# Attention sums of a graph layer on halves and quarters of TensorE's columns

## The chip, the cores and the metric

The kernel runs on one core of one Trainium2 chip. A core has a matrix engine (TensorE, PE in the profile; PEld are its weight loads), a vector engine (DVE), a scalar engine (ACT), GpSimd (POOL) and SyncE (SP), and DMA queues that SP, ACT and POOL issue to. The metric is the device time in microseconds of the core. Before the change the median of three runs is 1650.38 us (1650.38 to 1653.8).

## The reference, cut to what matters

The layer is a graph attention block followed by a mixture of eight expert networks, of which each token uses two. Everything is float32. The change concerns the attention:

```python
h = jnp.einsum('nd,hdk->hnk', x, W)                 # 4096 nodes, 4 heads, 64 columns each
s_col = jnp.einsum('hnk,hk->hn', h, a1)
s_row = jnp.einsum('hnk,hk->hn', h, a2)
e = jax.nn.leaky_relu(s_row[:, :, None] + s_col[:, None, :], negative_slope=0.2)
e = jnp.where(adj[None, :, :] > 0, e, NEG_INF)
att = jax.nn.softmax(e, axis=-1)
h_prime = jnp.einsum('hij,hjk->hik', att, h)
out = jnp.transpose(h_prime, (1, 0, 2)).reshape(N, OUT_DIM)
y = jax.nn.elu(out) + residual                      # then a layer norm
...
# experts: gate, top 2 of 8, gelu(xf @ W1[e] + b1[e]) @ W2[e] + b2[e], weighted sum
```

For each head and each node i the kernel needs two sums over the neighbours j: the sum of weight times row of h (64 numbers), and the sum of the weights (one number), by which the first is divided.

## The kernel before, in words

The 4,096 nodes i are cut into 8 blocks of 512 (B), and the neighbours j into 32 tiles of 128 (P). Block by block, `load_mask` brings a piece of the transposed adjacency matrix and turns it into a mask of zeros and ones on ACT (L778, L779). For each tile j, `weigh` makes four tiles w of 128 x 512 on DVE, one per head, with one instruction each (L786): the larger of a row term `er` and a column term `eb`, times the mask. These w rotate through ten buffers. `attend` then runs one matmul per head (L507): the stationary operand is `ha[:, j, h, :]`, 128 x 65, which holds the 64 columns of h scaled by a factor `ed` and, as column 65 (K1 = 65), the factor itself; the moving operand is w[h]; the result accumulates over the 32 tiles j in `acc[h]`, 65 partitions x 512 in one bank of PSUM per head. Row 65 of the result is the sum of weights. Each float32 matmul is carried out as two passes, each with its own weight load, so that the profile counts 2,048 where the program has 8 x 32 x 4 = 1,024.

In block 0 the norm of x (`norm_block`, transposes at L402) and the projections (`project_block`, L422 and L446, which also writes `ha`) are done tile by tile beside the attention. At the end of a block, `finish_block` copies the four accumulators from PSUM to `u` (two on ACT at L643, two on DVE at L645), transposes them in pieces of 65 x 128 back to nodes on partitions (L651, sixteen per block), copies each group of four to `raw` on ACT (L654), divides by the sum of weights (L659 to L667), and goes on with elu, residual, layer norm and routing (`route_block`). `finish_block` is a generator: its pieces are issued between tiles j of the next block, and those of the last block between pieces of the experts' work. The experts' stage (`up`, L889, and `down`, L902) reuses the PSUM banks acc0 to acc2 by turns for `up` and acc3 and ph for `down`.

There are two branches for the attention. The one under `general > 0` serves large scores; with these inputs the other one runs, and all lines of the profile are from it. Inside a branch a scheduler decides the order of the instructions on each engine from the program text, so that pieces of other work stand between the matmuls of L507. Each engine then works through its own list strictly as listed, and semaphores hold an instruction until what it reads is there or what it overwrites has been read.

The steps of the prediction touch `attend` (L505 to L509), `project_block` (L437), `finish_block` (L641 to L667), `up` (L886) and `down` (L900).

Of the kernel before, what the change touches and what calls it, by code (L numbers as in the profile page):

```python
# [9 lines left out]
F32 = mybir.dt.float32  # L10
# [3 lines left out]
OP = mybir.AluOpType  # L14
# [3 lines left out]
P = 128  # L18
# [9 lines left out]
TT = CH * NCH  # L28
# [9 lines left out]
def gat_then_moe(  # L38
# [19 lines left out]
    nc = tc.nc  # L58
    N, D = x.shape
    H, _, K = W.shape  # L60
    E, _, F = W1.shape
    NT = N // P
    DC = D // P
    FC = F // P
    B = 512
# [8 lines left out]

    W_1, W_2, ID, FIRST, RW = D, D + 1, D + 2, D + 3, D + 4
    TB = B // P
    K1 = K + 1
    HK = H * K

    const = ctx.enter_context(tc.tile_pool(name="const", bufs=1))  # L80
    small = ctx.enter_context(tc.tile_pool(name="small", bufs=3))
# [250 lines left out]
    with ExitStack() as layer:  # L332
# [46 lines left out]
        nc.vector.tensor_scalar(flag, wide, 0.5 * SPREAD, None, op0=OP.is_gt)  # L379


        ha = gat.tile([P, NT, H, K1], F32)
        sums = gat.tile([P, DC, NB], F32)
        eb = gat.tile([P, NT, H], F32)
        acc = [ps.tile([K1, B], F32, tag=f"acc{h}", name=f"acc{h}") for h in range(H)]

        turned = {}

# [21 lines left out]
        def project_block(b, apart):  # L410

            xT = turned[b]
            sc = small.tile([P, TB, 2 * H], F32, tag="sc", name="sc")
            rb = front.tile([P, TB, D], F32, tag="rb", name="rb", bufs=1)
            here = slice(b * TB, (b + 1) * TB)
            cols, rows = sc[:, :, :H], sc[:, :, H:]
            if not apart:
                nc.vector.memset(ha[:, here, :, K : K + 1], 1.0)
            for t in range(TB):
                ph = ps.tile([P, HK + 2 * H], F32, tag="ph", name="ph")  # L420
                for c in range(DC):
                    nc.tensor.matmul(  # L422
                        ph, xT[:, c, ts(t, P)], wall[:, c, :],
                        start=(c == 0), stop=(c == DC - 1),
                    )
                mine = ha[:, b * TB + t, :, :K]
                h4 = ph[:, :HK].rearrange("p (h k) -> p h k", h=H)
                if apart:
                    nc.vector.tensor_tensor(
                        sc[:, t, :H], ph[:, HK : HK + H], limit, OP.subtract  # L430
                    )
                    nc.vector.tensor_tensor(
                        sc[:, t, H:], ph[:, HK + H :], limit, OP.add
                    )
                    ed = ha[:, b * TB + t, :, K]
                    nc.scalar.activation(ed, sc[:, t, :H], AF.Exp, scale=SLOPE)
                    nc.vector.tensor_tensor(  # L437
                        mine, h4, ed.unsqueeze(2).to_broadcast([P, H, K]), OP.mult
                    )
                else:  # L440
                    nc.vector.tensor_copy(sc[:, t, :], ph[:, HK:])
                    nc.scalar.copy(mine, h4)
                if t % 2 == 0:
                    pr = ps.tile([P, 2, D], F32, tag="pr", name="pr")
                for c in range(DC):
                    nc.tensor.matmul(  # L446
                        pr[:, t % 2, :], xT[:, c, ts(t, P)], wr[:, c, :],
                        start=(c == 0), stop=(c == DC - 1),
                    )
                if t % 2:  # L450
                    nc.vector.tensor_tensor(
                        rb[:, t - 1 : t + 1, :], pr,
                        brm.unsqueeze(1).to_broadcast([P, 2, D]), OP.add,
                    )
            nc.gpsimd.dma_start(rows_of(residual, b), rb)

            part = small.tile([P, H, TB], F32, tag="part", name="part")
            turn = part.rearrange("p h t -> p t h")
            if apart:
                nc.scalar.activation(eb[:, here, :], cols, AF.Exp, scale=1.0 - SLOPE)  # L460
                nc.vector.tensor_scalar(turn, rows, 0.0, None, op0=OP.max)
                nc.scalar.activation(part, part, AF.Exp, scale=SLOPE - 1.0)
            else:
                nc.vector.tensor_copy(eb[:, here, :], cols)
                nc.vector.tensor_copy(turn, rows)
            pp = ps.tile([H * TB, P], F32, tag="ph", name="pp")
            nc.tensor.transpose(pp, part.rearrange("p h t -> p (h t)"), ident)
            sp = small.tile([H * TB, P], F32, tag="sp", name="sp")
            nc.scalar.copy(sp, pp)
            nc.gpsimd.dma_start(  # L470
                parts[:, ts(b, B)].rearrange("h (t p) -> h t p", p=P),
                sp,
            )
# [29 lines left out]
            return at  # L503

        def attend(w, j):  # L505
            for h in range(H):
                nc.tensor.matmul(  # L507
                    acc[h], ha[:, j, h, :], w[h], start=(j == 0), stop=(j == NT - 1)
                )  # L509

        def route_block(b, y):

# [118 lines left out]
        def finish_block(b):  # L631

            xb = fin.tile([P, TB, D], F32, tag="xf", name="xf", bufs=1)
            nc.sync.dma_start(xb, rows_of(x, b))
            nc.gpsimd.tensor_tensor(
                xb, xb, bet.unsqueeze(1).to_broadcast([P, TB, D]), OP.add
            )
            rb = fin.tile([P, TB, D], F32, tag="rb", name="rb", bufs=1)
            nc.sync.dma_start(rb, rows_of(residual, b))
            u = fin.tile([K1, H, B], F32, tag="u", name="u", bufs=1)  # L640
            for h in range(H):  # L641
                if h % 2 == 0:
                    nc.scalar.copy(u[:, h, :], acc[h])  # L643
                else:
                    nc.vector.tensor_copy(u[:, h, :], acc[h])  # L645
            yield
            raw = fin.tile([P, TB, H, K1], F32, tag="raw", name="raw", bufs=1)
            for t in range(TB):
                pt = ps.tile([P, H, K1], F32, tag="ptr", name="ptr", bufs=2)
                for h in range(H):  # L650
                    nc.tensor.transpose(  # L651
                        pt[:, h, :], u[:, h, ts(t, P)], ident[:K1, :K1]
                    )
                nc.scalar.copy(raw[:, t], pt)  # L654
                if t % 2:
                    yield
            shape = [P, TB, H, K]
            none = small.tile([P, TB, H], F32, tag="none", name="none")
            nc.vector.tensor_scalar(none, raw[:, :, :, K], 0.0, None, op0=OP.is_equal)  # L659
            z = small.tile([P, TB, H], F32, tag="z", name="z")  # L660
            nc.vector.tensor_tensor(z, raw[:, :, :, K], none, OP.add)
            nc.vector.reciprocal(z, z)
            y = fin.tile([P, TB, D], F32, tag="y", name="y", bufs=1)
            y4 = y.rearrange("p t (h k) -> p t h k", h=H)
            m = fin.tile([P, TB, D], F32, tag="m", name="m", bufs=1)
            m4 = m.rearrange("p t (h k) -> p t h k", h=H)
            nc.vector.tensor_tensor(  # L667
                y4, raw[:, :, :, :K], z.unsqueeze(3).to_broadcast(shape), OP.mult
            )
            nc.gpsimd.tensor_tensor(  # L670
                m4,
                hbar.unsqueeze(1).to_broadcast(shape),
                none.unsqueeze(3).to_broadcast(shape),
                OP.mult,
            )
            nc.gpsimd.tensor_tensor(y, y, m, OP.add)
            nc.vector.tensor_scalar(m, y, 0.0, None, op0=OP.min)
            nc.scalar.activation(m, m, AF.Exp)
            nc.vector.scalar_tensor_tensor(y, y, 0.0, m, op0=OP.max, op1=OP.add)
            yield  # L680
            nc.vector.tensor_tensor(y, y, rb, OP.add)
            yield
            mv, r = mean_rstd(y)
            for t in range(TB):
                nc.vector.scalar_tensor_tensor(  # L685
                    y[:, t, :], y[:, t, :], mv[:, t, 0:1], gam,
                    op0=OP.subtract, op1=OP.mult,
                )
            for t in range(TB):
                nc.vector.scalar_tensor_tensor(  # L690
                    y[:, t, :], y[:, t, :], r[:, t : t + 1], xb[:, t, :],
                    op0=OP.mult, op1=OP.add,
                )
            nc.gpsimd.dma_start(rows_of(out, b), y)
            yield
            yield from route_block(b, y)
# [185 lines left out]
    def up(job, xT):  # L882

        hT = work.tile([P, FC, TT], F32, tag="hT", name="hT")
        for f in range(FC):
            ph = ps.tile([P, TT], F32, tag=f"acc{turns[0] % 3}", name="ph")  # L886
            turns[0] += 1
            for c in range(DC):
                nc.tensor.matmul(  # L889
# [6 lines left out]
    def down(job, hT):  # L896

        yT = work.tile([P, DC, TT], F32, tag="yT", name="yT")
        for c in range(DC):
            py = ps.tile([P, TT], F32, tag=("acc3", "ph")[c % 2], name="py")  # L900
            for f in range(FC):
                nc.tensor.matmul(  # L902
                    py, job[2][:, f, ts(c, P)], hT[:, f, :],
# [101 lines left out]
```

## Time and profile before

| what | value |
|---|---|
| median of three runs | 1650.38 us |
| the profiled execution's own time, and its span | 1650.22 us, 1648.6 us |
| mean granted clock of TensorE | 0.981 |
| busy: PE, PE weight loads, DVE, ACT, POOL | 1541.9, 742.1, 1076.4, 485.5, 290.8 us |
| first and last start of the matmuls of L507 | 62.1 and 1049.3 us |
| busy in 60 to 1050 us: PE, DVE, ACT | 966.43, 917.00, 317.36 us |
| DMA over the span | 113 GB/s |

The span falls into two parts. From about 60 to 1050 us the attention runs; each block after the first takes about 119 us. From 1050 us on the experts run, with PE busy and DVE mostly idle. A group's row in the profile gives its line, engine, operation, tiles and shapes, then the busy time in us, the mean duration of one in ns, and the idle time of the engine just before it with what ended it. A matmul's duration includes the time until its result is out, which overlaps the next matmul: the busy time of the group is therefore less than count times mean.

### The profile page before, as it was taken

To read this page: it belongs to the slowest core of one execution; us is meant where nothing else is said; L and a number is where in the kernel's file an instruction comes from. 1 tells how busy PE (TensorE), PEld (TensorE's weight loads), DVE (VectorE), ACT (ScalarE), POOL (GpSimd) and SP (SyncE) were. 2 spreads that over 40 slices of the span, in tenths; PEclk is the share of its full clock that TensorE was granted. 3 is DMA by queue.
4 is the path that set the end of the run, shared out by engine and by line. 5 is a ranking of instruction groups with operands and counts; after the bars stand their busy time and mean duration, and the time that the engine had idled before them with its cause. 6 is when DMAs were issued, how large, how long until landed. Compare 5 with 4: busy or idle time off the path is not lost.

```text
span 1648.6 us, 14261 instructions
## 1 busy us (share of the span) xinstructions
PE 1541.9 (94%) x4886; PEld 742.1 (45%) x4886; DVE 1076.4 (65%) x2334; ACT 485.5 (29%) x611; POOL 290.8 (18%) x223
## 2 busy tenths in 40 slices
PE   4799999999999999999999999999499999999994
PEld 2354533333333333333333333467366666666662
DVE  4698789999999999899899899444111121221211
ACT  3343233332333223333323323343032222222220
POOL 1100010210210210211211111213412222222222
PEclk9899999999999999999999999999799999999997
DMA  5532223232332333423332311544565555566541
GB/s 171 142 118 89 77 77 115 93 111 90 105 112 91 112 92 102 126 68 105 126 102 94 96 64 42 188 140 111 139 184 136 135 138 136 141 155 153 154 109 20
DMA packets 120643, 187.93 MB, mean 114 GB/s; under 512 B 11525, under 2 KB 71877, under 8 KB 120557
## 3 DMA queue, kind: packets, MB, share of 16 engines
q1 hardware_dynamic: 92748, 148.03, 28.8%
q0 software_dynamic: 21120, 29.27, 8.2%
q10 hardware_dynamic: 6688, 9.58, 2.5%
q8 instruction: 42, 0.69, 0.2%
q14 instruction: 45, 0.36, 0.1%
HBM read 157.64 MB, written 29.18 MB: 113 GB/s over the span
## 4 chain that ended last, share of the span: by engine, by line
PE 77%; DVE 15%; DMA 4%; issue 1%; ACT 0%; POOLq 0%; POOL 0%; ACTq 0%; SPq 0%; DVEq 0%
PE acc L507 40%; PE ph L889 15%; PE py L902 15%; DVE w L786 9%; PE ph L422 2%; DMA out<-o,ids 1%; PE pr L446 1%; PE po L917 1%; DVE st L145 1%; DMA xb<-in_x 1%; PE pt L871 1%; PE pg L531 1%; DMA out<-y 1%; DVE y L690 1%; DVE y L685 1%
## 5 line engine op out<-in xcount | busy, mean ns | idle before, releaser
L507 PE MATMUL acc<-w,ha 128*65 128x512 f32 x2048 | 896.0, 594 | 21.9 <-DVE w L786 21.9
L786 DVE SCALAR_TENSOR_TENSOR w<-er,eb,am 128x512 f32<-128x512 f32 x1024 | 773.6, 776 | 48.7 <-PE acc L507 9.6
L507 PEld LDWEIGHTS acc<-w,ha 128*65 128x65 f32 x2048 | 277.5, 138 | 594.0 <-issue 360.1
L889 PE MATMUL ph<-xT,w 128*128 128x330 f32 x896 | 267.8, 447 | 5.5 <-DMA w<-in_L_ffn_W 3.4
L902 PE MATMUL py<-hT,w 128*128 128x330 f32 x896 | 255.8, 440 | 0.0
L778 ACT ACTIVATE am<-adj 128x2048 bf16<-128x2048 int32 x64 | 122.3, 1910 | 350.6 <-DVE w L786 348.1
L921 POOL DMA_INDIRECT out<-o,ids x84 | 133.3, 1586 | 406.5 <-DMA out<-o,ids 257.9
L902 PEld LDWEIGHTS py<-hT,w 128*128 128x128 f32 x896 | 168.6, 189 | 77.3
L889 PEld LDWEIGHTS ph<-xT,w 128*128 128x128 f32 x896 | 164.9, 191 | 76.5 <-issue 5.6
L906 DVE TENSOR_SCALAR yT<-py,bias 128x330 f32<-128x330 f32 x56 | 31.4, 561 | 246.7 <-PE py L902 246.7
L893 ACT ACTIVATE hT<-ph,bias 128x330 f32<-128x330 f32 x224 | 119.4, 536 | 166.2 <-PE ph L889 166.0
L626 POOL DMA_INDIRECT lists<-xe,at x64 | 73.8, 1152 | 341.1 <-DVE at L595 139.8
L779 ACT ACTIVATE am<-am 128x2048 bf16<-128x2048 bf16 x64 | 122.1, 1908 | 1.7
L875 ACT COPY xT<-pt 128x330 f32<-128x330 f32 x28 | 12.2, 434 | 238.7 <-PE pt L871 238.0
L918 DVE TENSOR_SCALAR o<-po,share 110x256 f32<-110x256 f32 x84 | 40.4, 481 | 39.1 <-PE po L917 39.0
L422 PE MATMUL ph<-wall,xT 128*128 128x264 f32 x128 | 36.9, 414 | 15.8 <-DVE ha L437 10.0
L670 POOL TENSOR_TENSOR m<-hbar,none 128x1024 f32<-128x1024 f32 x8 | 15.2, 1895 | 201.6 <-DVE none L659 201.6
L852 DVE TENSOR_TENSOR ids<-no,xr 110x3 int32<-110x3 f32 x14 | 2.3, 163 | 71.7 <-DMA xr<-lists 71.7
L845 DVE CAST ids<-xr 110x3 int32<-110x3 f32 x14 | 2.3, 167 | 67.5 <-DMA xr<-lists 65.8
L917 PE MATMUL po<-ident,yT 128*110 128x128 f32 x168 | 37.1, 280 | 3.4 <-DVE o L918 2.3
L871 PE MATMUL pt<-ident,xr 110*128 110x110 f32 x168 | 21.3, 263 | 17.6 <-DMA xr<-lists 17.6
L422 PEld LDWEIGHTS ph<-wall,xT 128*128 128x128 f32 x128 | 24.5, 201 | 27.7 <-issue 19.6
(208 smaller groups left out, 712.0 us busy)
## 6 DMA issues: line engine op xcount, KB each, us to landing
adj<-in_adj SPq DMA_DIRECT2D x64, 1024.0 KB
w<-in_L_ffn_W SPq DMA_DIRECT2D x56, 1024.0 KB
xr<-lists SPq DMA_DIRECT2D x28, 335.2 KB
er<-parts ACTq DMA_DIRECT2D x8, 1024.0 KB
xb<-in_x SPq DMA_DIRECT2D x8, 512.0 KB
residual<-rb POOLq DMA_DIRECT2D x8, 512.0 KB, 3.4
xf<-in_x SPq DMA_DIRECT2D x8, 512.0 KB
rb<-residual SPq DMA_DIRECT2D x8, 512.0 KB
```

The costliest lines, as they stand in the source:

```text
L422: nc.tensor.matmul(ph, xT[:, c, ts(t, P)], wall[:, c, :], start=(c == 0), stop=(c == DC - 1),)
L507: nc.tensor.matmul(acc[h], ha[:, j, h, :], w[h], start=(j == 0), stop=(j == NT - 1))
L626: nc.gpsimd.indirect_dma_start(lists, bass.IndirectOffsetOnAxis(ap=at[:, k, t : t + 1], axis=0), xe[:, t, :], None,)
L778: nc.scalar.activation(am, at, AF.Relu)
L779: nc.scalar.activation(am, am, AF.Sign)
L786: nc.vector.scalar_tensor_tensor(wh, er[:, h, :], eb[:, j, h : h + 1], am[:, j % TB, :], op0=OP.max, op1=OP.mult,)
L889: nc.tensor.matmul(ph, job[1][:, c, ts(f, P)], xT[:, c, :], start=(c == 0), stop=(c == DC - 1),)
L893: nc.scalar.activation(hT[:, f, :], ph, AF.Gelu, bias=job[3][:, f : f + 1])
L902: nc.tensor.matmul(py, job[2][:, f, ts(c, P)], hT[:, f, :], start=(f == 0), stop=(f == FC - 1),)
L917: nc.tensor.transpose(po[:, ts(c, P)], yT[:, c, ts(k, CH)], ident)
L918: nc.vector.tensor_scalar(o[:, k, :], po, job[5][:, k : k + 1], None, op0=OP.mult)
L921: nc.gpsimd.indirect_dma_start(out, bass.IndirectOffsetOnAxis(ap=job[4][:, k : k + 1], axis=0), o[:, k, :], None, compute_op=OP.add,)
```

## The change

The sum of rows and the sum of weights become separate matmuls. For the rows, the stationary operand is the 64 columns of one head alone, and the results of heads 0 and 1 go to partitions 0 to 63 and 64 to 127 of one accumulator (`acc[0]`), those of heads 2 and 3 to `acc[1]`: the first of each pair uses the left half of the columns of TensorE, the second the right half. For the weights, the stationary operand is the head's factor, repeated over 32 columns (`unit`), and the four heads' results go to the four quarters of a third accumulator, `den`. So there are eight matmuls per tile j in place of four. For even j the four of rows stand first in the program, for odd j the four of weights. At the end of a block there are three copies of 128 x 512 in place of four of 65 x 512, and twelve transposes of 128 x 128 in place of sixteen of 65 x 128; the sums of weights are transposed 32-fold and one of each 32 is kept (`total`). The experts' stage uses the banks acc0, acc1, den and a new bank `more`.

```diff
+    Q = 32
...
-        ha = gat.tile([P, NT, H, K1], F32)
+        ha = gat.tile([P, NT, HK], F32)
+        unit = gat.tile([P, NT, H], F32)
...
-        acc = [ps.tile([K1, B], F32, tag=f"acc{h}", name=f"acc{h}") for h in range(H)]
+        acc = [ps.tile([P, B], F32, tag=f"acc{i}", name=f"acc{i}") for i in range(H // 2)]
+        den = ps.tile([P, B], F32, tag="den")
...
-                mine = ha[:, b * TB + t, :, :K]
+                mine = ha[:, b * TB + t, :].rearrange("p (h k) -> p h k", h=H)
...
-                    ed = ha[:, b * TB + t, :, K]
+                    ed = unit[:, b * TB + t, :]
...
         def attend(w, j):
-            for h in range(H):
-                nc.tensor.matmul(
-                    acc[h], ha[:, j, h, :], w[h], start=(j == 0), stop=(j == NT - 1)
-                )
+            def rows():
+                for h in range(H):
+                    nc.tensor.matmul(
+                        acc[h // 2][ts(h % 2, K), :], ha[:, j, ts(h, K)], w[h],
+                        start=(j == 0), stop=(j == NT - 1),
+                    )
+
+            def weights():
+                for h in range(H):
+                    nc.tensor.matmul(
+                        den[ts(h, Q), :], unit[:, j, h : h + 1].to_broadcast([P, Q]), w[h],
+                        start=(j == 0), stop=(j == NT - 1),
+                    )
+
+            for do in (rows, weights) if j % 2 == 0 else (weights, rows):
+                do()
...
-            u = fin.tile([K1, H, B], F32, tag="u", name="u", bufs=1)
-            for h in range(H):
-                if h % 2 == 0:
-                    nc.scalar.copy(u[:, h, :], acc[h])
-                else:
-                    nc.vector.tensor_copy(u[:, h, :], acc[h])
+            u = fin.tile([P, 3, B], F32, tag="u", name="u", bufs=1)
+            nc.scalar.copy(u[:, 0], acc[0])
+            nc.vector.tensor_copy(u[:, 1], acc[1])
+            nc.scalar.copy(u[:, 2], den)
             yield
-            raw = fin.tile([P, TB, H, K1], F32, tag="raw", name="raw", bufs=1)
+            raw = fin.tile([P, TB, HK], F32, tag="raw", name="raw", bufs=1)
             for t in range(TB):
-                pt = ps.tile([P, H, K1], F32, tag="ptr", name="ptr", bufs=2)
-                for h in range(H):
-                    nc.tensor.transpose(
-                        pt[:, h, :], u[:, h, ts(t, P)], ident[:K1, :K1]
-                    )
-                nc.scalar.copy(raw[:, t], pt)
+                if t % 2 == 0:
+                    pt = ps.tile([P, 2, HK], F32, tag="ptr", name="ptr", bufs=2)
+                for i in range(H // 2):
+                    nc.tensor.transpose(pt[:, t % 2, ts(i, P)], u[:, i, ts(t, P)], ident)
                 if t % 2:
+                    nc.scalar.copy(raw[:, t - 1 : t + 1, :], pt)
                     yield
+            pd = ps.tile([P, TB, H, Q], F32, tag="ptr", name="pd", bufs=2)
+            for t in range(TB):
+                nc.tensor.transpose(
+                    pd[:, t].rearrange("p h q -> p (h q)"), u[:, 2, ts(t, P)], ident
+                )
+            total = small.tile([P, TB, H], F32, tag="total", name="total")
+            nc.scalar.copy(total, pd[:, :, :, 0])
...
-            ph = ps.tile([P, TT], F32, tag=f"acc{turns[0] % 3}", name="ph")
+            ph = ps.tile([P, TT], F32, tag=("acc0", "acc1", "den")[turns[0] % 3], name="ph")
...
-            py = ps.tile([P, TT], F32, tag=("acc3", "ph")[c % 2], name="py")
+            py = ps.tile([P, TT], F32, tag=("more", "ph")[c % 2], name="py")
```

More of the change, by code (lines that the diff above doesn't have):

```diff
@@ L76, in gat_then_moe @@
     TB = B // P
-    K1 = K + 1
     HK = H * K
+    Q = 32
     const = ctx.enter_context(tc.tile_pool(name="const", bufs=1))
@@ L417, in project_block @@
             if not apart:
-                nc.vector.memset(ha[:, here, :, K : K + 1], 1.0)
+                nc.vector.memset(unit[:, here, :], 1.0)
             for t in range(TB):
@@ L639, in finish_block @@
             nc.sync.dma_start(rb, rows_of(residual, b))
-            u = fin.tile([K1, H, B], F32, tag="u", name="u", bufs=1)
-            for h in range(H):
-                if h % 2 == 0:
-                    nc.scalar.copy(u[:, h, :], acc[h])
-                else:
-                    nc.vector.tensor_copy(u[:, h, :], acc[h])
+            u = fin.tile([P, 3, B], F32, tag="u", name="u", bufs=1)
+            nc.scalar.copy(u[:, 0], acc[0])
+            nc.vector.tensor_copy(u[:, 1], acc[1])
+            nc.scalar.copy(u[:, 2], den)
             yield
-            raw = fin.tile([P, TB, H, K1], F32, tag="raw", name="raw", bufs=1)
+            raw = fin.tile([P, TB, HK], F32, tag="raw", name="raw", bufs=1)
             for t in range(TB):
-                pt = ps.tile([P, H, K1], F32, tag="ptr", name="ptr", bufs=2)
-                for h in range(H):
-                    nc.tensor.transpose(
-                        pt[:, h, :], u[:, h, ts(t, P)], ident[:K1, :K1]
-                    )
-                nc.scalar.copy(raw[:, t], pt)
+                if t % 2 == 0:
+                    pt = ps.tile([P, 2, HK], F32, tag="ptr", name="ptr", bufs=2)
+                for i in range(H // 2):
+                    nc.tensor.transpose(pt[:, t % 2, ts(i, P)], u[:, i, ts(t, P)], ident)
                 if t % 2:
+                    nc.scalar.copy(raw[:, t - 1 : t + 1, :], pt)
                     yield
+            pd = ps.tile([P, TB, H, Q], F32, tag="ptr", name="pd", bufs=2)
[5 more added lines that the diff above has]
+            nc.scalar.copy(total, pd[:, :, :, 0])
             shape = [P, TB, H, K]
             none = small.tile([P, TB, H], F32, tag="none", name="none")
-            nc.vector.tensor_scalar(none, raw[:, :, :, K], 0.0, None, op0=OP.is_equal)
+            nc.vector.tensor_scalar(none, total, 0.0, None, op0=OP.is_equal)
             z = small.tile([P, TB, H], F32, tag="z", name="z")
-            nc.vector.tensor_tensor(z, raw[:, :, :, K], none, OP.add)
+            nc.vector.tensor_tensor(z, total, none, OP.add)
             nc.vector.reciprocal(z, z)
@@ L667, in finish_block @@
             nc.vector.tensor_tensor(
-                y4, raw[:, :, :, :K], z.unsqueeze(3).to_broadcast(shape), OP.mult
+                y4, raw.rearrange("p t (h k) -> p t h k", h=H), z.unsqueeze(3).to_broadcast(shape), OP.mult
             )
```

## The prediction

> **What bounds the kernel now.** I read the page's busy shares first, then the chain that ended last, then the groups, and then stretches of time, to see whether one limit holds in the whole attention.
>
> ```profile
> PE 1541.9 (94%) x4886; PEld 742.1 (45%) x4886; DVE 1076.4 (65%) x2334; ACT 485.5 (29%) x611; POOL 290.8 (18%) x223
> ...
> PE acc L507 40%; PE ph L889 15%; PE py L902 15%; DVE w L786 9%; PE ph L422 2%; DMA out<-o,ids 1%; PE pr L446 1%; PE po L917 1%; DVE st L145 1%; DMA xb<-in_x 1%; PE pt L871 1%; PE pg L531 1%; DMA out<-y 1%; DVE y L690 1%; DVE y L685 1%
> ...
> L507 PE MATMUL acc<-w,ha 128*65 128x512 f32 x2048 | 896.0, 594 | 21.9 <-DVE w L786 21.9
> L786 DVE SCALAR_TENSOR_TENSOR w<-er,eb,am 128x512 f32<-128x512 f32 x1024 | 773.6, 776 | 48.7 <-PE acc L507 9.6
> L507 PEld LDWEIGHTS acc<-w,ha 128*65 128x65 f32 x2048 | 277.5, 138 | 594.0 <-issue 360.1
> ```
>
> The first line says that PE is busy 94% of the span; the second that the matmuls of L507 are 40% of the path that ended last, and DVE's w only 9%. The third says that PE stood idle before L507 for 21.9 us in all. The weight loads (138 ns) lie beside the running matmuls.
>
> The next lines are busy time in stretches: one block of the attention, and the attention as a whole. The columns after the length are PE, PEld, DVE, ACT, POOL.
>
> ```profile
> 452.00:571.00 119.00, 115.31 (x304) 38.91 (x303) 112.51 (x204) 38.84 (x31) 16.18 (x12) 1.00 0.32 102
> 60.00:1050.00 990.00, 966.43 (x2627) 349.50 (x2628) 917.00 (x1765) 317.36 (x304) 130.56 (x97) 1.00 0.30 95
> ```
>
> PE is busy 966 of 990 us, DVE 917. DVE's figure misleads: its w stretch when they wait for a buffer. The timelines show the true paces.
>
> ```profile
> 644.44 13.93 PE L507 MATMUL acc<-w,ha 128*65 128x512 f32 x32
> ...
> 299.98 2.73 DVE L786 SCALAR_TENSOR_TENSOR w<-er,eb,am 128x512 f32<-128x512 f32 x4
> ...
> 309.54 10.02 DVE L786 SCALAR_TENSOR_TENSOR w<-er,eb,am 128x512 f32<-128x512 f32 x13
> ```
>
> 32 passes took 13.93 us, so one pass follows another after (13.93 - 0.594) / 31 = 0.430 us; a pass alone lasts 0.594, so 0.164 us of it is the run-out that the next pass normally covers. A w on DVE takes (2.73 - 0.74) / 3 = 0.66 us when nothing holds it, and (10.02 - 0.74) / 12 = 0.77 when PE does. Per tile j, PE needs 8 x 0.430 = 3.44 us and DVE 4 x 0.66 = 2.64 us. PE bounds the attention; DVE at its own pace would need 917 - 773.6 + 1024 x 0.66 = 819 us of the 990.
>
> **The change, part by part.**
>
> *The passes.* Removed: 2,048 passes, 2,048 x 0.430 = 881 us. Added: 4,096 passes (1,024 matmuls of rows and 1,024 of weights, two passes each), and everything turns on how many run at once. No operation of the trace uses part of the columns, so the price is bounded: without any overlap 4,096 x 0.430 = 1,761 us, that is +880; with columns never idle, 1,024 x 2 x 1/2 + 1,024 x 2 x 1/4 = 1,536 passes long, 660 us, that is -221 on PE, and then DVE would bound (below).
>
> What the built order of the new kernel says matters here. The program alternates four rows and four weights, but the scheduler has mixed them, because a w comes from DVE at a time: in the branch that runs, the 2,048 matmuls stand in 364 runs of rows (114 of one matmul, 117 of two, 58 of three, 8 of four, 16 of five, 18 of seven, 33 of eight) and 383 runs of weights (202 of one, 27 of two, 19 of three, 50 of four, 49 of five, 7 of six, 8 of seven, 21 of eight). A run of one has no partner. If matmuls of one kind on different columns run together, and different kinds don't, then a run of rows takes 2 passes per started pair: 2 x (114 + 117 + 2 x 58 + 2 x 8 + 3 x 16 + 4 x 18 + 4 x 33) = 1,230; a run of weights takes 2 passes per started four: 2 x (202 + 27 + 19 + 50 + 2 x (49 + 7 + 8 + 21)) = 936. Together 2,166 passes long, 931 us: **+50**. I take this value, between the ends: the halves and quarters do different work on different columns, which speaks for overlap within a kind.
>
> *The breaks.* Where the kind changes, the array has to change from halves to quarters or to the whole, and I take it that the old kind must run out first. The order has 822 such places (671 between rows and weights, 151 next to full-width work such as transposes). Each costs between 0 and the run-out plus an uncovered weight load, 0.164 + 0.138 = 0.302 us. I take the run-out, which is the nearest row: 822 x 0.164 = **+135** (ends 0 and +248).
>
> [...]
>
> *The end of a block.* Removed: 128 transposes of L651, eight in 0.66 us, so 10.6 us. Added: 96 of 128 x 128; the nearest row is L525, 64 in 10.4 us busy, 0.163 each, 15.6 us. **+5**, on PE. ACT loses 16 copies of `u` (581 ns) and 32 of `raw` (376 ns), 21.3 us, and gets 16 of `u`, 16 of `raw` (128 x 512, as `u`, 581 ns) and 8 of `total` (at most 376 ns), some 21.6: nothing, since ACT is busy 317 of 990 us; if ACT had no room it would be 0.3. The start of the next block waits for the copies of `acc`: block starts are even j, rows first, and those copies are first in line, as now. DVE loses 8 copies of 681 ns (-5.4 us) and gets 365 more semaphore instructions in the branch (494 against 129 in the built order; the median of those before L786 is 21 ns), +7.7 us. That hides behind PE: DVE would need 819 + 2 = 821 us. Uncovered, it would cost 2. No DMA is added or moved, and no queue of SP or POOL.
>
> *Before and after.* `project_block` writes the same numbers to another layout: nothing (uncovered, a few ns on 32 small writes). The experts' banks: `up` waits for acc0, acc1 and den, the last freed by ACT's second copy, as acc2 is now: 0, and bounded by PE's present idle time before L889, 5.5 us.
>
> **The sum:** 1650.22 (profiled execution: span 1648.6 and 1.6 around it) + 50 + 135 + 5 = **1840 us**. The execution lies 0.16 us below the median, so nothing is added. With the ends of the breaks, this case spans 1705 to 1955.
>
> **The rivals.**
>
> 1. *Strict order* (slower still). The two passes of a matmul stand next to each other on the same columns. If a pass can't start before the one listed ahead of it has started, the second head's first pass waits for the first head's second, and only neighbours overlap: a run of n takes n + 1 passes. 2,048 + 747 runs = 2,795 passes, 1,202 us, +321; with breaks 135 and transposes 5 it is 2111. For it: the trace shows PE working through its list in order. Against it: nothing that a row shows.
> 2. *Kinds coexist* (faster, the other side). Rows and weights on free columns run at the same time, no break is paid. PE's time is then between 660 and 931 us. Singles of weights stand between pairs of rows that fill both halves, so they seldom find room: two thirds up, 841, is -40, and +5 makes 1615. DVE's 821 us is the floor of the attention, so 1650 - (990 - 821) = 1481 is the most it could give. It decides as soon as the passes and breaks together take less than 881 - 5 = 876 us; even without breaks, runs of one kind (931) don't reach that, so the kinds themselves must overlap.
> 3. *No overlap at all:* the change doesn't do what it says. 4,096 passes one after another: +880 + 5, 2535 us (2670 with breaks). For it: the trace holds no two matmuls side by side. Against: separate columns and separate banks or partitions.
>
> **How the numbers follow.** My case 0.45, strict order 0.20, coexisting kinds 0.23, no overlap 0.10, no measurable change 0.02. A measurement of this kernel can tell about 0.2%, 3 us, from no change. Faster comes from rival 2 alone (0.23); slower is 0.45 + 0.20 + 0.10 = 0.75. The range leaves out rival 3 (0.10), the lower part of rival 2 (0.05) and the top of rival 1 (0.05): 1600 to 2120. My case alone has 1705 to 1955.
>
> **What the profile after would show.** If I am right: PE busy near all of an attention of about 1,180 us, a block of about 142 us, runs of weights of four in hardly more time than one, idle or stretched passes at each change of kind, and DVE waiting for PE (w's buffers) far longer than 48.7 us. Under strict order: starts of passes no closer than 0.43 us between heads except neighbours. Under coexistence: L786 the largest entry of the chain, blocks under 119 us. The prediction is wrong if a change of kind costs nothing, if passes of the same head's two halves hold up the others, or if DVE becomes the bound.

## The result, and the profile after

The changed kernel takes 1833.13 us (median of four runs, 1830.99 to 1837.53), the kernel before 1650.78 us in the same series. The ratio is 1.1104, with a 95% interval of 1.1078 to 1.1129: the change makes the kernel 11% slower. The forecast was 1840 us.

From the page of the changed kernel: busy shares, the chain that ended last by line, and the three costliest groups of the attention (L513 are the rows, L520 the weights, L807 DVE's w).

```profile
PE 1730.5 (94%) x6902; PEld 685.3 (37%) x6902; DVE 1045.7 (57%) x2326; ACT 483.1 (26%) x603; POOL 326.6 (18%) x223
...
PE acc L513 28%; PE den L520 23%; PE ph L910 13%; PE py L923 12%; DVE w L807 4%; PE ph L425 2%; DMA out<-o,ids 2%; PE pr L449 1%; PE po L938 1%; DMA xb<-in_x 1%; PE pg L548 1%; PE pt L892 1%; DVE z L682 1%; DVE st L145 1%; DVE y L706 1%
...
L807 DVE SCALAR_TENSOR_TENSOR w<-er,eb,am 128x512 f32<-128x512 f32 x1024 | 729.8, 760 | 107.7 <-PE den L520 71.9
L513 PE MATMUL acc<-w,ha 128*64 128x512 f32 x2048 | 623.0, 611 | 3.2 <-DVE w L807 2.9
L520 PE MATMUL den<-w,unit 128*32 128x512 f32 x2048 | 494.1, 604 | 14.5 <-DVE w L807 14.5
```

PE is as busy as before, 94%, and the matmuls of the attention are now 51% of the chain in place of 40%. DVE waits 107.7 us before its w (48.7 before), most of it for matmuls of weights to release a buffer. The attention's passes start at 61.7 and end their starts at 1232.5 us; before it was 62.1 to 1049.3. That is 183.6 us more, and the span grew by 184.2: all of the loss is in the attention. A block takes 142 us in place of 119. In busy time by stretches (PE, PE weight loads, DVE, ACT, POOL):

```profile
452.00:594.00 142.00, 139.73 (x552) 32.02 (x552) 106.76 (x201) 37.90 (x29) 21.63 (x12) 0.99 0.29 86
```

The timeline of PE shows how the time goes. Each line is a run of passes of one kind: start, length with the last pass's run-out, line and number of passes (two per matmul).

```profile
642.53 1.04 PE L520 MATMUL den<-w,unit 128*32 128x512 f32 x2
643.50 1.08 PE L513 MATMUL acc<-w,ha 128*64 128x512 f32 x4
644.51 1.91 PE L520 MATMUL den<-w,unit 128*32 128x512 f32 x12
646.35 1.07 PE L513 MATMUL acc<-w,ha 128*64 128x512 f32 x2
647.35 1.04 PE L520 MATMUL den<-w,unit 128*32 128x512 f32 x2
648.33 3.65 PE L513 MATMUL acc<-w,ha 128*64 128x512 f32 x14
651.91 1.92 PE L520 MATMUL den<-w,unit 128*32 128x512 f32 x14
```

From start to start: one matmul of weights takes 0.97 us (642.53 to 643.50), two of rows 1.01, one of rows 1.00, six of weights 1.84, seven of rows 3.58. So a second half is nearly free (two rows cost 0.01 us more than one), as are a second, third and fourth quarter: over the whole trace, from start to start, the median run of one weights matmul takes 0.975 us and of four 0.996; of one row 1.003, of two 1.009, of three 1.861, of four 1.868. Every run also carries about 0.12 (weights) or 0.15 us (rows) beyond its 2 x 0.428 us of passes: the change of kind. Of 747 runs of the attention, 202 are one matmul of weights alone and 114 one of rows alone, in which half or three quarters of the columns idle.

### The profile page after: what moved, and what is told of

It is laid out like the page before. It is cut to its first block, busy times and chain, and to the rows that moved or that the text cites. A ratio compares the mean times of both kernels' runs of the same rounds, so it can differ in the third digit from the quotient of the medians.

```text
span 1832.8 us, 18639 instructions
## 1 busy us (share of the span) xinstructions
PE 1730.5 (94%) x6902; PEld 685.3 (37%) x6902; DVE 1045.7 (57%) x2326; ACT 483.1 (26%) x603; POOL 326.6 (18%) x223
## 4 chain that ended last, share of the span: by engine, by line
PE 83%; DVE 8%; DMA 4%; issue 2%; POOL 0%; ACT 0%; POOLq 0%; SPq 0%; DVEq 0%
PE acc L513 28%; PE den L520 23%; PE ph L910 13%; PE py L923 12%; DVE w L807 4%; PE ph L425 2%; DMA out<-o,ids 2%; PE pr L449 1%; PE po L938 1%; DMA xb<-in_x 1%; PE pg L548 1%; PE pt L892 1%; DVE z L682 1%; DVE st L145 1%; DVE y L706 1%
## 5 line engine op out<-in xcount | busy, mean ns | idle before, releaser
L807 DVE SCALAR_TENSOR_TENSOR w<-er,eb,am 128x512 f32<-128x512 f32 x1024 | 729.8, 760 | 107.7 <-PE den L520 71.9
L513 PE MATMUL acc<-w,ha 128*64 128x512 f32 x2048 | 623.0, 611 | 3.2 <-DVE w L807 2.9
L520 PE MATMUL den<-w,unit 128*32 128x512 f32 x2048 | 494.1, 604 | 14.5 <-DVE w L807 14.5
L513 PEld LDWEIGHTS acc<-w,ha 128*64 128x64 f32 x2048 | 143.0, 136 | 453.1 <-issue 363.4
L520 PEld LDWEIGHTS den<-w,unit 128*32 128x32 f32 x2048 | 78.6, 107 | 360.0 <-issue 227.4
L643 POOL DMA_INDIRECT lists<-xe,at x64 | 105.8, 1654 | 422.0 <-DVE at L612 262.8
```

What stands on the lines that cost most here:

```text
L513: nc.tensor.matmul(acc[h // 2][ts(h % 2, K), :], ha[:, j, ts(h, K)], w[h], start=(j == 0), stop=(j == NT - 1),)
L520: nc.tensor.matmul(den[ts(h, Q), :], unit[:, j, h : h + 1].to_broadcast([P, Q]), w[h], start=(j == 0), stop=(j == NT - 1),)
L643: nc.gpsimd.indirect_dma_start(lists, bass.IndirectOffsetOnAxis(ap=at[:, k, t : t + 1], axis=0), xe[:, t, :], None,)
L807: nc.vector.scalar_tensor_tensor(wh, er[:, h, :], eb[:, j, h : h + 1], am[:, j % TB, :], op0=OP.max, op1=OP.mult,)
```

## The experiments

The streaming times below are worked out from the starts of all passes of the attention in a trace: each pass counts 0.428 us from its start (the passes of L507 in the kernel before follow each other at a median of 0.429), and overlapping stretches count once. What is left between the first and the last pass, I call the rest (breaks, other work of PE, waits). Where no interval is given below, the time is that of a single run. For the kernel before it is 876.5 us of streaming and 111.1 of rest; for the changed kernel 958.0 and 213.3.

**One kind of matmul: the weights in halves too.**

```diff
-    Q = 32
+    Q = 64
...
-                        den[ts(h, Q), :], unit[:, j, h : h + 1].to_broadcast([P, Q]), w[h],
+                        den[h // 2][ts(h % 2, Q), :], unit[:, j, h : h + 1].to_broadcast([P, Q]), w[h],
```

> Sums of weights also in halves (the factor repeated over 64 columns, two accumulators): as many matmuls as in the changed kernel, but all of one kind. In the built order the 2,048 matmuls stand in 68 runs, 135 breaks (all next to full-width work), 2,064 passes long. Theory (passes of one kind overlap, each break costs about 0.13 us): 2,064 x 0.4275 = 882 us of passes against 875 before, 135 x 0.13 = 18 us of breaks, 16 transposes of 128x128 per block for 16 of 65x128, about 8: 1650 + 7 + 18 + 8 = 1683 us. Rival (the number of matmuls, each with its own weight load, is what costs, not the changes of kind): no better than the changed kernel, 1833 us or above.

Measured: 1707.99 us, beside 1650.57 for the kernel before. The same 2,048 matmuls without a change of kind between rows and weights cost 125 us less than in the changed kernel, so the number of matmuls isn't what costs. But it is 25 above the sum. Its passes streamed for 918.8 us, not 882, at a mean of 1.91 at a time: now and then one half ran alone.

**All in quarters: a head's 64 columns as two matmuls of 32.**

```diff
-                for h in range(H):
+                for i in range(2 * H):
                     nc.tensor.matmul(
-                        acc[h // 2][ts(h % 2, K), :], ha[:, j, ts(h, K)], w[h],
+                        acc[i // 4][ts(i % 4, Q), :], ha[:, j, ts(i, Q)], w[i // 2],
...
```

> Rows in quarters too: each head's 64 columns as two matmuls of 32, twelve matmuls per tile j, all of one kind; 3,072 matmuls in 74 runs, 147 breaks, 1,584 passes long if the four quarters run at once. Theory: 1,584 x 0.4275 = 677 us and 147 x 0.13 = 19 us, with some 90 us of other work on PE 786 us, less than DVE's own 821: DVE becomes the bound and the attention takes 821 to 900 us in place of 990, so 1480 to 1560 us, taken at 1530. Rival (the number of matmuls costs): half as many again as in the changed kernel, so above 1833 us. Rival (a pass can't start before the one listed ahead of it): 3,072 + 74 passes, 1345 us, above 2100 us.

Measured: 1657.63 us, ratio to before 1.0037 (1.0024 to 1.0051). Three times as many passes as before (6,144) stream in 751.0 us, at a mean of 3.50 at a time, so both rivals fall, and PE isn't the bound any more. But it is 128 us above the 1530 that I took. Where most of them went, the lists of DVE's and PE's waits and the timeline of one block's end show (in waits: who waits for whom, total us, times, longest; in the timeline: start, length, and in brackets the idle time before):

```profile
DVE m L698 <- POOL y L697: 87.5, 7, 14.8
PE acc L513 <- DVE w L807: 85.0, 14, 13.1
```

```profile
536.92 25.39 POOL L643 DMA_INDIRECT lists<-xe,at  x1 [1.75 <-DMA lists<-xe,at]
571.18 11.91 POOL L643 DMA_INDIRECT lists<-xe,at  x1 [8.86 <-DMA lists<-xe,at]
...
597.28 0.96 POOL L643 DMA_INDIRECT lists<-xe,at  x1 [1.74 <-DMA lists<-xe,at]
598.26 1.91 POOL L691 TENSOR_TENSOR m<-hbar,none 128x1024 f32<-128x1024 f32 x1
600.25 2.34 POOL L697 TENSOR_TENSOR y<-y,m 128x1024 f32<-128x1024 f32 x1
602.62 0.69 DVE L698 TENSOR_SCALAR m<-y 128x1024 f32<-128x1024 f32 x1 [14.33 <-POOL y L697]
```

GpSimd issues the indirect DMAs that write a block's routed rows, then does two element-wise steps of the next block's end. One of these issues takes 25.39 us here and another 11.91, so the steps come late; DVE stands 14.33 us before L698, whose input the second step writes, and makes its next w only after it, at 603.23 us, so that PE runs dry: its waits for w are about as long (85.0 us). That happens in seven blocks. The granted clock of TensorE is 0.96 over this attention (60 to 1042 us; 1.00 before, 0.50 in the wait from 595.4 to 602.1 us); it is 0.99 in the next run of quarters below, where the waits are gone. What this clock cost the passes here was not shown; in the changed kernel, passes of L513 that ran while 0.50 was granted (412.8 to 416.2 us) took up to 1.116 us in place of the median 0.592.

**The same matmuls as in the changed kernel, in the order of the program.** Each matmul of `attend` is queued behind the one before it (an order on PE's list only, no wait):

```diff
+                with tc.issue_after(tail[0]):
+                    made = go()
...
+            for do in (row, weight) if j % 2 == 0 else (weight, row):
+                for h in range(H):
+                    do(w, j, h)
```

> The changed kernel's own matmuls, but issued in the order of the program (each held behind the one before it in the list): four rows, four weights, four weights, four rows. 339 runs instead of 747, 421 breaks instead of 822, 1,606 passes long instead of 2,166. Theory: 1,606 x 0.4275 = 687 and 421 x 0.13 = 55 us, with 90 us of other work on PE 832 us, about DVE's 821: attention 850 to 930 us, so 1510 to 1590 us, taken at 1560: faster than before. Rival (number of matmuls, or halves and quarters as such): as the changed kernel, about 1833 us, since the work is the same.

Measured: 1641.22 us, 192 us below the changed kernel, with the same matmuls on the same columns. So the loss lies in the order in which they stand. It streams for 753.1 us (687 expected) and is 81 us above the 1560 that I took; of DVE's waits, 50.8 us are for the same y of GpSimd, which accounts for most of it:

```profile
DVE m L702 <- POOL y L701: 50.8, 7, 9.1
```

**The same matmuls, pinned in pairs: two rows, two weights.**

```diff
+            for h in range(0, H, 2):
+                for do in (row, weight):
+                    for i in range(h, h + 2):
+                        do(w, j, i)
```

> The changed kernel's own matmuls pinned in pairs: two rows, two weights, two rows, two weights. 1,054 runs and 1,134 breaks instead of 822, 2,108 passes long, about as many as the changed kernel's 2,166. Theory: -58 x 0.4275 = -25 us and +312 x 0.13 = +41 us: 1849 us. Rival (a break costs nothing, only lost partners do): 1833 - 25 = 1808 us.

Measured: 1834.93 us, 14 below the theory and 27 above the rival. Streaming fell by 27.6 us to 930.4, the rest rose by 22.3 to 235.6. Breaks cost something, then, but less than the 0.13 us I used: against the kernel before, (235.6 - 111.1) / 1,134 = 0.11 us each here, and (213.3 - 111.1) / 822 = 0.12 in the changed kernel (the 5 us of larger transposes included).

**Quarters, with GpSimd's two steps on DVE.**

```diff
-            nc.gpsimd.tensor_tensor(
+            nc.vector.tensor_tensor(
                 m4,
...
-            nc.gpsimd.tensor_tensor(y, y, m, OP.add)
+            nc.vector.tensor_tensor(y, y, m, OP.add)
```

> All in quarters, and the two element-wise steps of finish_block that ran on GpSimd (m and y of 128x1024) on DVE instead. Theory (with PE no longer the bound, DVE runs its w without a pause, GpSimd's indirect DMAs stretch to as much as 25 us, and DVE stood waiting for y behind them, 87.5 us in seven blocks): the waits go, DVE gets 14 instructions of 1.2 us, 17 us: 1656 - 87.5 + 17 = 1585 us. Rival (those waits only stand where DVE or PE would have waited anyway, or return at GpSimd's next step, xf or the store of y): 1640 to 1660 us.

Measured: 1583.43 us, ratio to before 0.9581 (0.9564 to 0.9598). The waits are gone from DVE's list, and the sum of the two terms is met within 2 us. GpSimd's issues are as slow as in the run of quarters above (294.3 us for 64), but no wait for GpSimd is left in DVE's list:

```profile
L643 POOL DMA_INDIRECT lists<-xe,at x64 | 294.3, 4599 | 358.6 <-DMA lists<-xe,at 163.8
```

In its middle blocks DVE is now busy 116.77 of 119 us:

```profile
452.00:571.00 119.00, 113.01 (x877) 45.23 (x869) 116.77 (x227) 40.20 (x31) 53.27 (x14) 1.00 0.36 113
```

**The pinned order, with the two steps on DVE.** The edits of the pinned order and of the last run together.

> The changed kernel's own matmuls in the pinned order, with the same two steps moved to DVE. Theory: its waits for y were 50.8 us, so 1641 - 51 + 17 = 1607 us. Rival (the waits return elsewhere): 1630 to 1650 us.

Measured: 1604.46 us, 3 below the theory. So with their order and the two steps put right, the changed kernel's matmuls take 3% off the time of before (1652.8 in this series), and 2.4% off the kernel before with the same two steps moved (next).

**The kernel before, with the two steps on DVE.** The same edit of `finish_block`, on the kernel before.

> The kernel before with the two steps moved to DVE and nothing else. Theory (PE bounds it, DVE has room): 1650 us within 5. Rival (GpSimd's lateness cost the kernel before as well, and the gain of the moved versions is not due to the matmuls): about 1585 to 1610 us. Rival (DVE is as full as its busy share says): 1650 + 19 = 1669 us.

Measured: 1643.77 us in one run, 9 below the median of before and 7 below its lowest run (1650.57). It is more than the nothing I expected, but far from 1585: moving the two steps doesn't give the gain of the two versions above by itself, nor do the quarters (1657.63 us); it takes both. The few us show in the rest, which falls from 111.1 to 101.0 us: in it, PE's waits for w fall from 21.9 to 10.1.

**Quarters, head by head and pinned.** Each head's two quarters of rows, then its weights on a third quarter, so that one w feeds three matmuls (with the weights' quarters in another order, ACT's copy of `total` becomes four):

```diff
+        place = (2, 0, 3, 1)
...
+            put(den[ts(place[h], Q), :], unit[:, j, h : h + 1].to_broadcast([P, Q]), w[h], j)
...
+            for h in range(H):
+                row(w, j, h)
+                weight(w, j, h)
```

> All in quarters, head by head (two quarters of rows, then the weights on a third quarter), pinned in that order, with the two steps on DVE. 1,586 passes long as in e7_quarters_moved, but each head's three matmuls follow its w. Theory (DVE bounds, so a better order of PE's work gives little): 1575 to 1590 us. Rival (in e7_quarters_moved PE still waits on badly placed matmuls): 20 us or more below it.

Measured: 1588.22 us, ratio 0.9604 (0.9585 to 0.9623), not below the unpinned quarters. Where DVE bounds, this order on PE gains nothing.

**More buffers for w: the changed kernel, one kind, and the best version.** Against the version that each starts from, only this line is different:

```diff
-                        wh = work.tile([P, B], F32, tag="w", name="w", bufs=10)
+                        wh = work.tile([P, B], F32, tag="w", name="w", bufs=16)
```

> The changed kernel with sixteen buffers for w in place of ten, nothing else. Its order has 822 breaks and is 2,160 passes long, as the changed kernel's (822 and 2,166). Theory (the order on PE, its runs and breaks, sets the time): 1833 us within 10. Rival (each w is now held for two matmuls, so ten buffers are too few, and DVE's 71.9 us of waiting for den is what is lost): 1760 us or below.

Measured: 1828.57 us. DVE's idle time before its w fell from 107.7 to 44.4 us, and the kernel gained 5:

```profile
L807 DVE SCALAR_TENSOR_TENSOR w<-er,eb,am 128x512 f32<-128x512 f32 x1024 | 727.0, 762 | 44.4 <-PE den L520 22.6
```

DVE's waits in the changed kernel are a consequence, not the cause.

> All in halves (e1_one_kind) with sixteen buffers for w. That run came out at 1708 us, 25 above its sum: its passes streamed for 919 us in place of 882, so at times only one half ran. Theory A (PE waits within a run for the next w, because DVE can't run far enough ahead with ten buffers): back towards the sum, 1683 to 1695 us. Theory B (the order of the list lets one half run dry, whatever DVE does): 1708 us within 5.

Measured: 1705.19 us, as theory B says, but for neither reason alone. The passes did come closer together (899.8 us of streaming in place of 918.8), while the rest rose from 123.0 to 142.6. PE now waits for the routing's normed rows, a wait that isn't in the list of the run with ten buffers:

```profile
PE ptx L542 <- DVE xe L533: 21.9, 7, 3.4
```

This wait is about as long as the growth of the rest, so what the buffers gained seems to be given back there. Why what L542 reads comes later than PE needs it was not tested.

> All in quarters, the two steps on DVE (e7_quarters_moved, 1583 us), sixteen buffers for w. DVE bounds there, its waits for buffers are under 10 us: theory 1575 to 1585 us. Rival (PE's waits for w, 33 us, come from DVE standing in other waits that more buffers would cover): 1550 to 1570 us.

Measured: 1580.18 us, ratio 0.9571 (0.9555 to 0.9587), the same as with ten buffers. DVE bounds it.

## Why the prediction was right

- *PE bounds the attention.* Right before, and in the changed kernel (the chain gives its matmuls 51%), as the sixteen buffers show: they take away 63 of the 107.7 us that DVE waits before its w, and the time stays within 5 us.
- *Passes of one kind on different columns overlap.* Right, and the step that mattered most. Two halves take 1.009 us where one takes 1.003, four quarters 0.996 where one takes 0.975. The strict-order rival needs five passes, 2.14 us, for a run of four weights, and the no-overlap rival eight; both fall.
- *The order decides: 364 and 383 runs.* Right. The order's runs are the trace's runs, and pinning the same matmuls in longer runs takes 192 us away.
- *The passes, +50.* Too small: streaming rose from 876.5 to 958.0, by 82. Some 18 of the missing 32 us of streaming stand in two kinds of run whose matmuls come apart because they wait: 18 runs of seven rows took 76.0 us in all, against 18 x 3.577 if the shortest of them is the rule, and 21 runs of eight weights 51.3 against 21 x 1.853. In most of the stretched ones PE waits for a w from DVE. But six of the runs of seven rows stand across the start of a block, and there the next rows wait first for the copies of the accumulators (ACT L658, then DVE L659) and then for a w behind DVE's copy: 0.8 us each. The prediction had put the block's start at nothing, since the copies are "first in line, as now". The sum had counted only passes and no waiting inside a run. (The prediction's bounds rest on "No operation of the trace uses part of the columns"; L507 itself fills 65 of them, and what no row showed is two matmuls side by side.)
- *The breaks, +135.* Too large: the rest rose by 102, so 0.12 us each in place of the 0.164 of the whole run-out. From the last pass of a run to the first of another kind it takes 0.523 us in place of 0.428, so 0.095 of the run-out stays uncovered; and the first pass before the second is 0.052 us longer in a run of rows and 0.025 in one of weights. (Its upper end is 1840 - 135 + 248 = 1953, not 1955.) The two errors, -32 and +33, cancel by luck, so that the total is nearer than its terms deserve. That the old kind must run out first was the author's assumption, which no row of before shows; what the runs show is this 0.095 of the 0.164 us.
- *The block's end, +5; DVE's extra semaphores, nothing.* Not seen apart: the transposes went from 10.8 to 15.4 us of busy time, and DVE had room.
- *Rival 2, kinds coexist.* Its mechanism doesn't happen: at none of the 671 changes does a run of the other kind begin sooner than 0.522 us after the last pass's start. A gain is to be had in another way, with few changes of kind and GpSimd's two steps moved; one kind in halves alone (1707.99 us) gives none.
- *DVE's floor of 821 us for the attention.* Too low. The best versions reach an attention of about 903 us from the first pass to the last. With the quarters and the two steps on DVE, DVE is busy 865.86 of the 906 us from 60 to 966: its w took 707.3 us, 0.69 each in place of 0.66, the moved steps some 17, and 40 us it stood idle. Where the steps stayed on GpSimd, the wait for y came on top (87.5 us). The floor had counted none of these.

## What to carry to other kernels

Matmuls on separate halves or quarters of the columns ran at the same time here at almost no extra cost (two halves 1.009 us where one took 1.003, four quarters 0.996 where one took 0.975), but each change between halves, quarters and the full width cost about 0.12 us and left unpaired matmuls alone: look at the order that a scheduler makes of it, since the written order isn't what runs, and keep the columns full and the changes few. One width for all isn't enough by itself: all in halves took 1707.99 us, two widths in the pinned order 1641.22, all in quarters 1657.63; with the two steps moved, the pinned order took 1604.46 and all in quarters 1583.43. When the bounding engine is relieved, look at what is queued in order behind the slowest issuer on another engine; here moving two small steps off GpSimd turned the version in quarters from one worth nothing (1.0037) into one worth 4% (0.9581), while on the kernel before the same move gave 9 us in one run.

## What the hardware showed that I had not expected

The list gives the two passes of a head next to each other on the same columns; I had thought it possible that this keeps the next head waiting. It doesn't: in a run of eight weights the first four passes start within 0.02 us and the next four 0.452 us after the first, so passes on other columns start ahead of a pass that stands before them in the list and waits for its own columns. The trace shows this without the list, too: in the run of eight weights at 684.8 us the last head waits for its w until 2.161 us into the run, and the three heads before it start their first passes at 0.882, 0.888 and 0.895 us and their second ones at 1.311, 1.317 and 1.324. If the list goes head by head, first passes have overtaken the second pass of the head before; if it has first passes in front, the second ones have overtaken the waiting one. Between different columns, starts don't keep the order that the rival of strict order supposes, nor the "strictly as listed" of the kernel's description; line by line PE's starts keep it (880 stretches of one line in the attention's branch of the changed kernel come in the built order), as do those of PE and DVE in the kernel before (187 and 1,052).

An indirect DMA's issue on GpSimd took a mean of 1152 ns in the kernel before, 1654 in the changed one, 4563 with all in quarters. In the slowest one of the latter, DVE was busy 25.19 of 25.39 us; in a like stretch of the kernel before, eight issues took 8.36 us in all while DVE was busy 22.19 of 25.25 us. First all in quarters, then before (columns as above):

```profile
536.92:562.31 25.39, 25.39 (x224) 12.21 (x218) 25.19 (x40) 11.05 (x8) 25.39 (x1) 1.00 0.30 89
```

```profile
543.25:568.50 25.25, 25.25 (x60) 8.14 (x59) 22.19 (x31) 7.32 (x4) 8.36 (x8) 1.00 0.38 121
```

So of these two stretches, the one in which DVE hardly pauses is the one in which GpSimd hardly gets on. DVE's timeline beside the issue that ends at 562.31 us (536.92 + 25.39) ties the two closer:

```profile
535.55 25.93 DVE L807 SCALAR_TENSOR_TENSOR w<-er,eb,am 128x512 f32<-128x512 f32 x39
561.68 0.69 DVE L659 COPY u<-acc 128x512 f32<-128x512 f32 x1 [0.20 <-PE acc L513]
```

39 w follow each other without a pause, and the issue ends 0.84 us after the last of them. The five other issues of 24 to 25.4 us in this run end in the same way, and of 118 issues of over 3 us in the traces of all runs 91 end 0.83 to 0.86 us after the first w in them that no other w follows at once.

None of the runs changes DVE's pauses by themselves, so that DVE's unbroken work is what holds these issues up is argued, not shown; nor does a run show by what means.
